# A macaron block on one core: the second batch's last shared-expert products, ahead of the expert tiles or inside them

## The chip, the cores and the metric

The kernel runs on one NeuronCore of a Trainium2 chip. The metric is the device time of one execution in microseconds; a kernel's time is the median of several executions. A core has TensorE (PE, matrix products), VectorE (DVE), ScalarE (ACT), GpSimd (POOL) and SyncE (SP), each with its own instruction queue; DMA engines move data between HBM and the on-chip memory. TensorE writes its results to PSUM, which has eight banks here.

## The reference

Input x has 4 batches of 512 rows with 256 columns, float32. Three half-steps follow one another, each on a layernorm without weights:

```
x = x + 0.5 * ffn(layernorm(x))
x = x + attention(layernorm(x))
x = x + 0.5 * ffn(layernorm(x))

ffn(x):   scores = sigmoid(x @ gate_w); the 2 best of 16 experts (by scores + bias), weights normed to sum 1
          shared = (silu(x @ shared_gate_w) * (x @ shared_up_w)) @ shared_down_w
          routed = sum over the two experts of weight * ((silu(g) * u) @ down[e]),  g, u = halves of x @ gate_up[e]
          return shared + routed
attention(x): 3 heads of 256; the softmax runs over the query axis; the heads' mean goes through fc_w, fc_b
```

There is one shared expert, which every row passes, and 16 routed experts with an inner width of 128. "Second shared expert" in the change's name is the shared expert on the second batch, x1.

## The kernel before

Rows are sorted by expert through memory. For each batch of 512 rows the kernel computes the layernorm, its transpose and the router's scores; finds for each row its two experts and its place among that expert's rows; and scatters the normed rows into a buffer `xn_d` in HBM, in which each expert has a region of its own (`router`, lines 359 to 445, GpSimd's indirect DMAs at line 438). Behind the last row of each region some blank rows are written (`blanks`, line 470). Then the routed experts run in tiles of 128 rows, all of one expert each: 40 tiles always, more only if the routing needs them.

`experts` (lines 621 to 699) is that loop, software-pipelined by hand. Step i does, in program order: load the rows of tile i (`load`, SyncE, line 569), transpose them on TensorE (`turn`, PSUM tile `pxt`, copied to `xt` by ScalarE); the gate and up products of tile i-1 (`up`, PSUM `peg`, with `sig` on ScalarE and two products on VectorE that give `eh`); the transpose of `eh` for tile i-2 (`flip`, PSUM `pht`, copied to `hT` by VectorE); the down product of tile i-3 (`down`, PSUM `pey`, scaled by ScalarE into `ey` and scattered to `y_d` in HBM by GpSimd, line 671). At given steps a function is called at the end of the step: the dictionary `at`. With the constants here, `DONE[0]` is 25, `late` is 37, and `NA[0]` is 40 tiles.

The first 9 tiles (`NF`) need only rows of the first three batches, so their table (`early`) is found before the last batch has been scattered. The table of the others is `table` (lines 547 to 559, on VectorE), and their loads wait for the blank rows.

The shared expert is three functions. `shared_up` (line 581): the two products of a batch, 128 x 512 each, in PSUM tiles `pg` and `pu` of tag "mm". `shared_gate` (line 594): two VectorE products, giving `h`. `shared_down` (line 600): four products of `h` with `shared_down_w` in two PSUM tiles `po` of tag "dn" (line 605; TensorE takes each float32 product in two passes, so the trace has 8 rows for it), and for each `po` one VectorE instruction that adds half of it to x (line 609). In the first half-step this is done for batches 0 and 1 ahead of the tiles, for batches 2 and 3 after them.

PSUM is shared out by tag: three banks for "mm" (`pg`, `pu`, `peg`, `pey`, the attention's products), three for "dn" (`pxt`, `pht`, `po`, the transposes of the layernorm), one each for the router's two. A tile gives its bank back when its last reader is done.

What sets the order. The framework's scheduler orders each engine's queue when the program is built: of the instructions that are ready it takes the first in program order. The kernel steers it in three ways. `in_turn` (line 224) ties groups of instructions on one engine, such as TensorE's groups ahead of the tiles, into a fixed sequence; "D0_1" is the name of the four products of `shared_down(1)`. `after` ties one instruction behind another of its engine; the argument `behind` of `shared_down` puts the VectorE sums of line 609 behind a given instruction. `tc.issue_after` does so for all that a block issues on that engine.

Before the change the order on VectorE at the end of the stage ahead is: `early`, `shared_gate(1)`, the two sums of batch 0, the two sums of batch 1, `table`. On TensorE it is: the groups C0_0 to C0_3 (counts), G2, Ug0_1 and Uu0_1 (`shared_up(1)`), D0_1, then the tiles.

Of the kernel before, what the change touches and what calls it, by code (L numbers as in the profile page):

```python
# [21 lines left out]
def tile_macaron_block(  # L22
# [51 lines left out]
    NA = [NK * NT + NE // 2, NK * NT + NE // 2 + 2]  # L74
# [141 lines left out]
    behind = const.tile([P, NB], F32, tag="behind", name="behind")  # L216
# [79 lines left out]
    class Ffn:  # L296
# [433 lines left out]
        def add(self, b, js=slice(0, NJ), behind=None):  # L730
            for yg in self.got[b]:
                ins = nc.vector.tensor_tensor(xs[b][:, js], xs[b][:, js], yg[:, js], ALU.add)  # L732
                if behind is not None:
                    after(ins, behind)


    ffn = Ffn(0)
# [68 lines left out]
        ffn.early()  # L806
    with tc.issue_after(ffn.last.ins):
        ffn.shared_gate(1)
    ffn.shared_down(0, behind=ffn.last)
    done = ffn.shared_down(1, behind=ffn.last)  # L810
    with tc.issue_after(done.ins):
        ffn.table()

    in_turn(
        "Z0", "Tln0_0", "Z1", "S0_0", "Tln0_1", "Z2", "K0_0", "Z3", "L0_0", "S0_1", "A0", "Ug0_0", "Uu0_0",
        "K0_1", "Tln0_2", "A1", "L0_1", "S0_2", "A2", "Tln0_3", "S0_3", "F", "K0_2", "L0_2", "G0",
        "D0_0", "G1", "K0_3", "L0_3", "C0_0", "C0_1", "C0_2", "C0_3", "G2", "Ug0_1", "Uu0_1", "D0_1",
    )

    in_turn(  # L820
# [8 lines left out]
    def add(f, b, j):  # L829
        return lambda: f.add(b, slice(j, j + 1), f.flips[-1])  # L830


    late = DONE[0] + 12
    ffn.experts(0, NA[0], {late - 10: ffn.ask, late: lambda: ffn.fetch_y(0)} | {
        late + 1 + j: add(ffn, 0, j) for j in range(NJ)
    })

# [201 lines left out]
    behind = ffn2.last  # L1039
# [39 lines left out]
```

## Time and profile before

| | |
|---|---|
| time, median of 4 runs | 509.76 us (507.44 to 510.96) |
| the profiled execution's own time | 512.11 us |
| its span, first to last instruction | 510.3 us |
| mean granted TensorE clock | 0.972 |
| stage ahead of the tiles | to about 57 us |
| first half-step's tiles | about 57 to 128 us |
| attention, three batches' routers in it | to about 400 us |
| second half-step's tiles | about 400 to 490 us |

In the profile's views, L605 is line 605 of the kernel; `po<-sd,h` names the tiles that an instruction writes and reads, without their numbers; x8 is the count of a merged row. The bracket behind a row is the idle time of that engine before it and what ended it. PE are TensorE's products, SPq the DMA queue that SyncE feeds, PEclk or the clock column the share of full clock that TensorE was granted. Ends of products are modelled: a product's row lasts longer than its share of a dense sequence, so the price of one in a sequence is taken from start to start.

### The profile page before, as it was taken

The page shows a single profiled execution, that of the slowest core. Times are in us where ns is not written, and L with a number is a line of the kernel's source. Part 1 is how long each engine was busy: PE and PEld are TensorE (multiplying, and loading weights), DVE is VectorE, ACT ScalarE, POOL GpSimd, SP SyncE. Part 2 cuts the span into 40 slices and gives each one's busy share as a digit, 9 for nine tenths or more (in the row PEclk, how much of TensorE's full clock was granted, in tenths as well). Part 3 has the DMA queues.
Part 4 walks back from the last instruction along what each step waited for, and adds up shares of the span by engine and source line. Part 5 has one row for each costly group of instructions (what it writes and reads, how often), then busy time and mean ns, then how long its engine had stood idle before and what let it go on. Part 6 is the DMA issues. An engine that isn't in the chain of part 4 may idle for free. (4 is left out here: it accounts for less than half of the span.)

```text
span 510.3 us, 7948 instructions
## 1 busy us (share of the span) xinstructions
PE 481.2 (94%) x2262; PEld 373.7 (73%) x2262; DVE 294.9 (58%) x981; ACT 224.5 (44%) x514; POOL 235.2 (46%) x281
## 2 busy tenths in 40 slices
PE   7988789999998999999999999999999889999985
PEld 3676478887566788678885778867888567888843
DVE  5856835556886922467406893325935475455565
ACT  3563256665436730456204664044640323666630
POOL 2377765665684140530256502644006067555543
PEclk9887999999999999999999999999999979999989
DMA  7996676566300000000022000200002327656756
GB/s 254 350 376 210 190 270 184 166 193 222 115 0 1 1 0 1 0 1 1 2 84 82 1 1 0 74 11 1 1 2 83 94 84 242 193 161 214 238 188 207
DMA packets 34734, 57.39 MB, mean 112 GB/s; under 512 B 4928, under 2 KB 25408, under 8 KB 34688
## 3 DMA queue, kind: packets, MB, share of 16 engines
q1 hardware_dynamic: 25424, 32.99, 21.3%
q0 software_dynamic: 8160, 23.44, 12.6%
q10 hardware_dynamic: 1104, 0.42, 0.3%
q8 instruction: 20, 0.33, 0.3%
q14 instruction: 26, 0.21, 0.2%
HBM read 30.78 MB, written 26.05 MB: 111 GB/s over the span
## 5 line engine op out<-in xcount | busy, mean ns | idle before, releaser
L671 POOL DMA_INDIRECT y_d<-ey,to x82 | 79.6, 970 | 53.6 <-ACT xt L632 43.3
L438 POOL DMA_INDIRECT xn_d<-xn_ln,pos x64 | 62.2, 972 | 86.6 <-DVE fa L489 23.0
L644 PE MATMUL peg<-gu,xt 128*128 x328 | 86.8, 389 | 3.0 <-DVE g L597 1.6
L970 PE MATMUL pa<-v,ex 128*128 128x256 f32 x384 | 86.2, 382 | 0.0
L970 PEld LDWEIGHTS pa<-v,ex 128*128 128x128 f32 x384 | 71.6, 190 | 9.2
L644 PEld LDWEIGHTS peg<-gu,xt 128*128 128x128 f32 x328 | 57.2, 194 | 10.3 <-issue 3.5
L661 DVE COPY hT<-pht 128x128 f32<-128x128 f32 x82 | 23.8, 290 | 55.2 <-PE pht L659 55.1
L666 PE MATMUL pey<-dn,hT 128*128 x164 | 49.3, 383 | 1.4 <-DVE hT L661 1.4
L670 ACT ACTIVATE ey<-pey,xg 128x256 f32<-128x256 f32 x82 | 38.9, 474 | 23.3 <-PE pey L666 21.8
L929 PE MATMUL pv<-G,xnT_lna 128*128 128x256 f32 x192 | 43.5, 382 | 2.7 <-ACT v L938 2.1
L868 PE MATMUL py<-xnT_lna,A 128*128 128x512 f32 x96 | 42.7, 593 | 1.0 <-DVEq L710 1.0
L929 PEld LDWEIGHTS pv<-G,xnT_lna 128*128 128x128 f32 x192 | 36.0, 190 | 9.6 <-ACT v L938 3.3
L905 ACT ACTIVATE ex<-ex,nmax 128x512 f32<-128x512 f32 x48 | 34.2, 714 | 18.5 <-DVE nmax L903 18.4
L650 ACT ACTIVATE sig<-peg 128x128 f32<-128x128 f32 x82 | 22.8, 278 | 41.4 <-PE peg L644 39.4
L975 DVE TENSOR_TENSOR x<-x,pa 128x256 f32<-128x256 f32 x16 | 6.7, 420 | 50.1 <-PE pa L970 45.3
L632 ACT COPY xt<-pxt 128x256 f32<-128x256 f32 x82 | 29.9, 366 | 12.0 <-PE pxt L628 8.8
L872 ACT COPY y<-py 128x512 f32<-128x512 f32 x24 | 13.8, 581 | 46.1 <-PE py L868 46.0
L628 PE MATMUL pxt<-ident,xg 128*128 128x128 f32 x164 | 31.8, 275 | 2.3 <-DVE xnT_ln L292 0.8
L868 PEld LDWEIGHTS py<-xnT_lna,A 128*128 128x128 f32 x96 | 18.2, 190 | 20.6 <-issue 19.8
L881 POOL TENSOR_TENSOR right<-y 128x256 f32<-128x256 f32 x12 | 10.0, 833 | 50.0 <-ACT y L872 50.0
L250 ACT ACTIVATE std_ln<-mv_ln,eps 128x4 f32<-128x4 f32 x8 | 2.4, 297 | 65.3 <-DVE mv_ln L248 65.2
L628 PEld LDWEIGHTS pxt<-ident,xg 128*128 128x128 f32 x164 | 22.5, 141 | 11.7 <-ACT xt L632 1.3
(201 smaller groups left out, 891.1 us busy)
## 6 DMA issues: line engine op xcount, KB each, us to landing
xg<-xn_d SPq DMA_DIRECT2D x82, 129.0 KB, 2.3
gu<-ffn_experts_gate_up_dram SPq DMA_DIRECT2D x4, 1024.0 KB, 14.2
yg<-y_d SPq DMA_DIRECT2D x8, 512.0 KB, 3.8
y<-y_d SPq DMA_DIRECT2D x6, 512.0 KB, 5.2
dn<-_L_ffn_experts_down_dram SPq DMA_DIRECT2D x2, 1024.0 KB, 15.2
x<-in_L_attn_x_dram SPq DMA_DIRECT2D x3, 512.0 KB, 7.8
out_dram<-x SPq DMA_DIRECT2D x3, 512.0 KB
y_d<-ey,to POOLq DMA_INDIRECT x82, 2.8
```

What stands on the lines that cost most here:

```text
L438: ins = nc.gpsimd.indirect_dma_start(out=self.xn_v[k * NT + b * NJ + j], out_offset=bass.IndirectOffsetOnAxis(ap=pos[:, k, j : j + 1], axi ...
L628: ins = nc.tensor.transpose(pt[:, c, :], xg[:, c * P : (c + 1) * P], ident)
L632: nc.scalar.copy(xt, pt)
L644: nc.tensor.matmul(pg, xt[:, c, :], gu[:, bass.ds(e, 1), c, :], start=(c == 0), stop=(c == NC - 1),)
L661: self.flips.append(nc.vector.tensor_copy(hT, pt))
L666: self.downed = nc.tensor.matmul(py, hT, dn[:, bass.ds(e, 1), :], start=True, stop=True)
L670: nc.scalar.mul(y, py, xg[:, H + 1 : W])
L671: ins = nc.gpsimd.indirect_dma_start(out=self.y_v[i], out_offset=bass.IndirectOffsetOnAxis(ap=tos[i], axis=0), in_=y, in_offset=None,)
L868: nc.tensor.matmul(py, A[h][:, c, fc * P : (fc + 1) * P], xnT[:, c, :], start=(c == 0), stop=(c == NC - 1),)
L905: nc.scalar.activation(ex[:, m, :], ex[:, m, :], AF.Exp, bias=nmax[:, m : m + 1], accum_out=z[:, m : m + 1],)
L929: nc.tensor.matmul(pv, xnT[:, c, m * P : (m + 1) * P], G[h][:, c, :], start=(c == 0), stop=(c == NC - 1),)
L970: nc.tensor.matmul(pa, es[h][:, m, j * P : (j + 1) * P], vs[h][:, m, :], start=(h == 0 and m == 0), stop=(h == NH - 1 and m == NJ - 1),)
```

## The change

The four products and the two VectorE sums of `shared_down(1)` are no longer issued ahead of the tiles. They are issued at the end of the tiles' step 34 (`late - 3`), the sums behind the copy `hT` that was issued last (`f.flips[-1]`, that of tile 32). The table now follows the sums of batch 0, and "D0_1" is no longer a member of the fixed TensorE sequence.

```diff
     with tc.issue_after(ffn.last.ins):
         ffn.shared_gate(1)
-    ffn.shared_down(0, behind=ffn.last)
-    done = ffn.shared_down(1, behind=ffn.last)
+    done = ffn.shared_down(0, behind=ffn.last)
     with tc.issue_after(done.ins):
         ffn.table()
...
-        "D0_0", "G1", "K0_3", "L0_3", "C0_0", "C0_1", "C0_2", "C0_3", "G2", "Ug0_1", "Uu0_1", "D0_1",
+        "D0_0", "G1", "K0_3", "L0_3", "C0_0", "C0_1", "C0_2", "C0_3", "G2", "Ug0_1", "Uu0_1",
     )
...
+    def down(f):
+        return lambda: f.shared_down(1, behind=f.flips[-1])
+
 
     late = DONE[0] + 12
-    ffn.experts(0, NA[0], {late - 10: ffn.ask, late: lambda: ffn.fetch_y(0)} | {
+    ffn.experts(0, NA[0], {late - 3: down(ffn), late - 10: ffn.ask, late: lambda: ffn.fetch_y(0)} | {
         late + 1 + j: add(ffn, 0, j) for j in range(NJ)
     })
```

No DMA, no buffer and no tile size changes; the sums are the same.

## The prediction

> **What bounds the kernel now.** I read the page first: the busy times and the row of slices.
>
> ```profile
> span 510.3 us, 7948 instructions
> PE 481.2 (94%) x2262; PEld 373.7 (73%) x2262; DVE 294.9 (58%) x981; ACT 224.5 (44%) x514; POOL 235.2 (46%) x281
> PEclk9887999999999999999999999999999979999989
> ```
>
> TensorE (PE) is busy 94% of the span, and its granted clock falls only in the stage ahead of the tiles and once near slice 32. An average says nothing of the two places that the change touches, so I read the timeline there. First the end of the stage ahead (start, duration, engine, line, tiles, count, and in brackets the idle time before and who ended it):
>
> ```profile
> 52.78 1.02 PE L587 MATMUL pu<-xnT_ln,su 128*128 128x512 f32 x2
> 54.46 5.32 SPq L569 DMA_DIRECT2D xg<-xn_d  x6
> 54.95 2.00 DVE L609 SCALAR_TENSOR_TENSOR x<-po,x 128x512 f32<-128x512 f32 x3
> 55.09 1.99 PE L605 MATMUL po<-sd,h 128*128 128x256 f32 x8 [1.28 <-DVE h L598]
> 57.12 0.69 DVE L609 SCALAR_TENSOR_TENSOR x<-po,x 128x512 f32<-128x512 f32 x1 [0.17 <-PE po L605]
> 57.15 0.41 PE L628 MATMUL pxt<-ident,xg 128*128 128x128 f32 x2
> 57.73 0.16 DVE L489 TENSOR_SCALAR na<-psr 128x16 f32<-128x16 f32 x1
> 57.90 0.41 PE L628 MATMUL pxt<-ident,xg 128*128 128x128 f32 x2 [0.34 <-DVE na L489]
> ```
>
> The row of 55.09 is the group that moves (D0_1). Of the four L609 instructions the last two are its own; the table (from L489 `na`) starts behind them. The first tile's rows were asked for at 54.46; the shortest landing of an `xg` in this stretch is 2.2 us, the median 2.6, so tile 0 could not begin before 56.66, and it began at 57.15. Then the two ends of the tile stage:
>
> ```profile
> SPq L569 <- DMA xn_d<-blank,end: 7.2, 1, 7.2
> 73.25 0.44 PE L628 MATMUL pxt<-ident,xg 128*128 128x128 f32 x2 [0.65 <-DMA xg<-xn_d]
> 76.00:100.00 24.00, 24.00 (x135) 20.23 (x134) 12.31 (x59) 14.84 (x45) 14.40 (x15) 1.00 0.59 173
> 114.47 0.38 PE L628 MATMUL pxt<-ident,xg 128*128 128x128 f32 x2
> 116.10 0.38 PE L628 MATMUL pxt<-ident,xg 128*128 128x128 f32 x2
> ```
>
> The first is from the waits of SyncE's queue: the load of tile 9, the first that needs the blank rows, waits 7.2 us for them, goes out at 71.01, and TensorE idles 0.65 us until 73.25. The blanks stand behind GpSimd's scatters, which follow one another every 1.27 us from 49.47 to 65.71 without waiting for DVE or TensorE. So tile 9 has an appointment that the change does not touch. From there TensorE is never idle (24.00 of 24.00 us, third row) and a step takes 116.10 - 114.47 = 1.63 us: **before tile 9 a saving is swallowed, behind it every TensorE microsecond counts**.
>
> **What leaves the stage ahead.** Eight TensorE rows (four float32 products, two passes each) and two L609. No DMA moves, and nothing of SyncE's or GpSimd's queue is passed. TensorE is free from 53.80, but tile 0 waits for its landing: a gain between 0 and 57.12 - 56.66 = 0.46 us; tile 1 began 0.34 us after TensorE could, about 2.4 us after its own load, so I take 0.2. The table starts two L609 earlier, 1.4 us, and so no longer stands in front of the second tile's `eh`: about 0.2 us. Both gains, 0.4, end in the appointment at 73.25: worth nothing by themselves.
>
> **What the stage ahead loses.** D0_1 was also the only dense TensorE work between 53.80 and 58.72, when the first tile's expert products start. Without it that stretch of 4.9 us holds two transposes of 0.41. Rows of this trace show what such a stretch does (windows: length, TensorE busy and count, granted clock, DMA share, GB/s; then the timeline):
>
> ```profile
> 36.00:38.00 2.00, 2.00 (x18) 1.00 1.06 374
> 38.00:40.00 2.00, 0.62 (x12) 0.52 1.10 389
> 40.00:42.00 2.00, 1.32 (x3) 0.50 1.06 362
> 56.00:58.00 2.00, 1.59 (x8) 1.00 0.79 222
> 40.68 3.78 PE L762 MATMUL pwG<-fcT,w 128*128 128x256 f32 x8 [2.06 <-ACT fcT L798]
> 46.30 1.89 PE L762 MATMUL pwG<-fcT,w 128*128 128x256 f32 x8
> ```
>
> After a few microseconds of small products and a 2.06 us pause the clock went to 0.50 and eight equal rows took 3.78 instead of 1.89 us. In windows of 0.4 us the half clock lasts 3.4 us once (31.2 to 34.6) and 6.8 us three times (10.7, 38.1, 410.1); the last began inside a pause of 1.55 us. So I expect the clock to fall around 56 to 59. Here a rule speaks against the change: the Trainium skill, "TensorE: Matmul & The Clock Gate", Part 1, says the clock halves after an idle window of about 3.4 us and recovers after a busy one, and its table of practice advises no idle gap above about 3 us. Taken literally it would leave 53.80 to 57.15 undecided at 3.35 us, so 0 or 1.7 us; the rows above are stricter, since pauses of 2.06 and 1.55 us among light work were enough.
>
> Price: 3.4 us at half clock, where TensorE has work throughout (58.7 to 62.0), cost 1.7 us of work; where it falls earlier, on time that TensorE waits away, 0.5 to 1. Against it stand the 0.4 gained and the 0.65 of waiting at tile 9: 1.7 - 1.05 = 0.65 at most for a single 3.4 us, nothing at least. For 6.8 us: 3.4 - 1.05 = 2.35. Ends 0 and 2.35; I take **0.45**, near the single window, as eight tiles of dense work follow.
>
> **What step 34 pays.** Eight rows at (1.89 - 0.38) / 7 = 0.216 us each are 1.73; the group's own row gives (1.99 - 0.38) / 7 = 0.23, 1.84. I take **1.75**, all on the path, at about 116.1, between step 34's `pey` and step 35's `pxt`. Nothing hides it: a step has no TensorE idle time. DVE takes two L609, 2 x 0.69 = 1.38; its own work in a step is 0.29 + 0.28 + 0.29 + 0.15 = 1.01 of 1.63, and a step of 3.4 us holds 2.4. Waits added: each L609 waits for its pair of products (the 0.17 above) behind the copy `hT` of tile 32; queued behind it on DVE are `sig`, `eh`, `to` and `hT` of the next tiles, for which TensorE would wait. The two `po` also hold two of three PSUM banks of tag "dn": the first is free 0.86 + 0.17 + 0.69 = 1.72 us after it starts, the second at about 1.73 + 0.17 + 0.69 = 2.6, while the flip of tile 33 and the transposes of tile 36 that take these banks come after 1.73 + 0.22 + 0.87 = 2.8 and 3.4. So nothing; at most 0.7, from the second half's shared expert inside tiles, where pxt at 425.32 to pxt at 436.06 is 10.74 us: three steps (4.88), its rows (3.43 + 1.71) and 0.7 of stall. x1 is next read at 135.10, so the later sum is late for nobody. All that follows (the adds behind flips 36 to 39, the layernorm, the attention) hangs on the tiles' end and shifts with it; the next batch's fetch at 119.45 waits for tile 30, ahead of step 34.
>
> **Sum.** -0.4 ahead, swallowed; +0.45 at tile 9 by the clock; +1.75 at step 34: **+2.2 us**. The profiled execution took 512.11 (510.3 span, 1.8 around it): 514.3. It lies 2.35 above the median of the runs, 509.76 (507.44 to 510.96), to which I carry the difference: **512.0**, 0.43% slower, within the 0.5% that a measurement can tell from no change.
>
> **The rivals.**
> - *The clock stays up* or its loss fits whole into the 0.65: +1.75, **511.5**. For: the landing may bring tile 0 early. Against: the light stretch is longer than those that cost the clock. 0.15.
> - *Slower*: the half clock lasts two windows, 6.8 us, as three of four times here; tile 9 is then over its appointment by 2.35, and with 1.75 that is +4.1, **513.9**; a bank stall of 0.7 would make 514.6. It decides from the point where tiles 0 to 8 lose more than 1.05 us. Against: dense tiles follow from 58.7. 0.18.
> - *The gain gets through*: the 0.46 + 0.2 + 0.65 reach the tile stage, if blanks land earlier because DVE and TensorE have less to do: 1.75 - 1.3 = +0.45, **510.2**. Against: GpSimd's even 1.27 us. 0.08.
> - *The products don't run at step 34*: only the DVE sums are tied to it, and the matmuls may be ordered into an earlier gap. Then they cost TensorE nothing, but hold two of three banks, and a step becomes 0.94 (`pxt` until its copy ends) + 0.60 (`pht`) + two handovers of 0.1, 1.74 instead of 1.63, for some 25 steps: 0 to +2.8, say **511.2**. Against: the third shared expert's L587 products, whose operands were copied by 35.9, passed no earlier tile and started at 128.54. 0.07.
>
> **How the numbers follow.** The forecast has 0.52, with +1.7 (511.5) to +2.9 (512.7). The range 509.6 to 514.3 takes in all rivals but the end of the slower one, and the scatter of the runs. Slower by over 0.5% (above 512.3): a third of the forecast, 0.17, and the slow rival, 0.18, with 0.02 of the last: 0.37. Faster by as much needs 507.2, which no case gives; 0.03 for what I don't see. The rest, 0.60, is within 0.5%.
>
> **What would show it.** After: L605 with eight rows near 116, pxt to pxt there 3.4 us; windows from 56 to 62 with a clock of 0.5; tile 9's pxt at 73.3 to 74, its idle time gone; `na` at about 56.3. I am wrong if the clock stays at 1.00, if tile 9 moves ahead of 73, or if the step with the products costs clearly more than 1.75.

## The result and the profile after

| | before | after |
|---|---|---|
| time, median | 510.06 us (507.14 to 513.58, 76 runs) | 512.09 us (510.52 to 515.95, 50 runs) |
| ratio | | 1.0037, 95% interval 1.0026 to 1.0048 |
| span of the profiled execution | 510.3 us | 509.3 us |
| mean granted TensorE clock of the runs | 0.979 (79 runs beside the experiments) | 0.973 |

By the ratio the change costs 1.9 us (1.3 to 2.4). The two profiled executions say the opposite, 510.3 and 509.3: one execution is not the kernel. The group `pg`, the first products of the second batch's shared expert, starts at 50.21 us in the one and at 47.45 in the other, before anything that the change touches. So all that follows is measured from this anchor inside the same execution, and only the medians of many runs are compared as totals. The anchor and the first expert products (`peg`) in TensorE's timeline of before:

```profile
50.21 1.88 PE L587 MATMUL pg<-xnT_ln,sg 128*128 128x512 f32 x4
...
58.72 1.10 PE L644 MATMUL peg<-gu,xt 128*128 x4 [0.41 <-ACT xt L632]
```

The page of the kernel after, in the rows that the prediction read:

```profile
span 509.3 us, 7948 instructions
...
PEclk9988899999999999999999999999999889999997
```

The instruction count is that of before, 7948; nothing was added or lost. The end of the stage ahead, from the timelines after the change:

```profile
47.45 1.88 PE L587 MATMUL pg<-xnT_ln,sg 128*128 128x512 f32 x4
...
51.62 7.49 SPq L569 DMA_DIRECT2D xg<-xn_d  x9
52.16 1.28 DVE L609 SCALAR_TENSOR_TENSOR x<-po,x 128x512 f32<-128x512 f32 x2
53.36 0.17 DVE L489 TENSOR_SCALAR na<-psr 128x16 f32<-128x16 f32 x1
53.75 0.44 PE L628 MATMUL pxt<-ident,xg 128*128 128x128 f32 x2 [2.70 <-DMA xg<-xn_d]
55.72 0.41 PE L628 MATMUL pxt<-ident,xg 128*128 128x128 f32 x2 [1.53 <-DVE tiles L559]
56.55 2.04 PE L644 MATMUL peg<-gu,xt 128*128 x4 [0.42 <-ACT xt L632]
```

Two L609 are left, the table's `na` follows them at once, and L605 is gone: TensorE waits 2.70 us for the first tile's rows and 1.53 for the second's. The second bracket names `tiles`, a result of the table, but in the kernel the transposes of the first nine tiles read nothing of the table. The second load went out at 52.49 and loads in this stretch landed after 2.1 to 4.3 us, which fits 55.72. Then the price: four `peg` rows take 2.04 us; before, four took 1.10. The windows of the same execution name the reason (length, TensorE busy and count, the other engines, granted clock, DMA share, GB/s), and the last row is the dense stretch behind tile 9:

```profile
56.00:58.00 2.00, 1.58 (x6) 1.21 (x5) 0.17 (x1) 0.37 (x1) 1.70 (x2) 0.51 0.97 239
58.00:60.00 2.00, 2.00 (x9) 1.63 (x8) 0.94 (x6) 0.65 (x2) 1.39 (x3) 0.64 0.95 268
...
76.00:100.00 24.00, 24.00 (x135) 20.29 (x134) 12.28 (x60) 15.08 (x45) 14.10 (x16) 1.00 0.59 174
```

The clock is at a half from 56 to 59.4 us, 3.4 us long; before it was 1.00 there. Tile 9, from SyncE's waits and TensorE's timeline:

```profile
SPq L569 <- DMA xn_d<-blank,end: 7.9, 1, 7.9
```

```profile
70.65 0.38 PE L628 MATMUL pxt<-ident,xg 128*128 128x128 f32 x2
...
113.37 1.89 PE L605 MATMUL po<-sd,h 128*128 128x256 f32 x8
115.10 0.38 PE L628 MATMUL pxt<-ident,xg 128*128 128x128 f32 x2
```

SyncE still waits for the blank rows, but TensorE no longer does: tile 9 at 70.65 has no bracket. From `pg` to tile 9 it took 23.20 us, before 23.04: the half clock ate what leaving out the products had given, and the 0.65 us that TensorE had waited at tile 9. At step 34 the eight rows of L605 stand where they were put; from their start to the next `pxt` is 115.10 - 113.37 = **1.73 us**. And VectorE in that step:

```profile
114.44 0.69 DVE L609 SCALAR_TENSOR_TENSOR x<-po,x 128x512 f32<-128x512 f32 x1 [0.42 <-PE po L605]
115.30 0.69 DVE L609 SCALAR_TENSOR_TENSOR x<-po,x 128x512 f32<-128x512 f32 x1 [0.17 <-PE po L605]
116.49 0.29 DVE L661 COPY hT<-pht 128x128 f32<-128x128 f32 x1 [0.50 <-PE pht L659]
```

VectorE is idle before the next copy: the sums hold nobody up. Tile 9 to tile 39 is 49.36 us before and 50.96 after; from tile 39 to the end of the span it is 387.69 in both. So from `pg` on this execution is 1.76 us longer: 0.16 ahead of tile 9, 1.60 between tiles 9 and 39, where step 34 is, and nothing behind.

### The profile page after: what moved, and what is told of

Same layout as the page of the kernel before. It is cut to its first block, busy times and chain, and to the rows that moved or that the text cites. A ratio compares the mean times of both kernels' runs of the same rounds, so it can differ in the third digit from the quotient of the medians.

```text
span 509.3 us, 7948 instructions
## 1 busy us (share of the span) xinstructions
PE 478.7 (94%) x2262; PEld 372.4 (73%) x2262; DVE 296.4 (58%) x981; ACT 224.4 (44%) x514; POOL 235.3 (46%) x281
## 3 DMA queue, kind: packets, MB, share of 16 engines
q1 hardware_dynamic: 25424, 32.99, 21.4%
## 5 line engine op out<-in xcount | busy, mean ns | idle before, releaser
L644 PE MATMUL peg<-gu,xt 128*128 x328 | 88.3, 394 | 2.3 <-DVE g L597 1.6
L874 ACT COPY y<-py 128x512 f32<-128x512 f32 x24 | 13.8, 581 | 46.1 <-PE py L870 46.0
## 6 DMA issues: line engine op xcount, KB each, us to landing
yg<-y_d SPq DMA_DIRECT2D x8, 512.0 KB, 4.1
y<-y_d SPq DMA_DIRECT2D x6, 512.0 KB, 4.7
x<-in_L_attn_x_dram SPq DMA_DIRECT2D x3, 512.0 KB, 7.1
out_dram<-x SPq DMA_DIRECT2D x3, 512.0 KB, 5.3
```

What stands on the lines that cost most here:

```text
L644: nc.tensor.matmul(pg, xt[:, c, :], gu[:, bass.ds(e, 1), c, :], start=(c == 0), stop=(c == NC - 1),)
```

## The experiments

The theory (T) in its final form at the start: ahead of the tiles the gain, tile 9's wait and the half clock about cancel; step 34 is paid in full. Rivals: the half clock is dear and step 34 cheap; or the half clock costs nothing; or the gain ahead could be had by moving the blank rows. This table holds all kernels that ran where the kernel before takes some 510 us: e10_base and e11_both_zero on one such chip, the other experiments on another, each experiment's ratio to the kernel before on the same chip. The segments come from the one profiled execution of each, the ratio and the mean clock from its timed runs (10 to 12 each, 50 of the kernel after).

| kernel | ratio to before, 95% | mean clock | half-clock windows of 3.4 us at tiles 0 to 4 | `pg` to tile 9 | idle at tile 9 | tile 9 to 39 |
|---|---|---|---|---|---|---|
| before | | 0.979 | 0 | 23.04 | 0.65 | 49.36 |
| after | 1.0037 (1.0026 to 1.0048) | 0.973 | 1 | 23.20 | 0 | 50.96 |
| e1_left_out | 1.0039 (1.0015 to 1.0063) | 0.974 | 2 | 24.67 | 0 | 48.94 |
| e2_extra | 1.0033 (1.0004 to 1.0062) | 0.979 | 0 | 22.98 | 0.55 | 50.96 |
| e11_both_zero | 1.0046 (1.0021 to 1.0071) | 0.978 | 0 | 22.09 | 0 | 50.95 |
| e3_warm | 1.0041 (1.0017 to 1.0066) | 0.978 | 0 | 23.65 | 1.04 | 51.07 |
| e10_base | 0.9994 (0.9968 to 1.0020) | 0.979 | 0 | 23.48 | 1.57 | 49.41 |
| e4_blanks_first | 1.0086 (1.0058 to 1.0114) | 0.975 | 1 | 26.33 | 0 | 48.82 |
| e12_step4 | 1.0028 (1.0001 to 1.0055) | 0.975 | 2 | 25.89 | 0 | 49.25 |
| e13_drain | 1.0061 (1.0035 to 1.0086) | 0.971 | 1 | 23.22 | 0.84 | 49.51 |

**Step 34 alone: e2_extra and e11_both_zero.** Both leave the products ahead of the tiles and issue them once more at step 34; in e2_extra both sums count, in e11_both_zero the sums ahead are multiplied by 0.0, so its values are those of the kernel after.

```diff
+    again = ffn.up[1]
     done = ffn.shared_down(1, behind=ffn.last)
+    ffn.up[1] = again
...
-    ffn.experts(0, NA[0], {late - 10: ffn.ask, late: lambda: ffn.fetch_y(0)} | {
+    ffn.experts(0, NA[0], {late - 3: down(ffn), late - 10: ffn.ask, late: lambda: ffn.fetch_y(0)} | {
```

> The kernel before, with the products and sums of shared_down(1) both ahead of the tiles and again at step 34, so that x1 gets the shared part twice: this times the step 34 part alone. My theory (eight rows at 0.216 us with nothing to hide them, no stall): +1.75 us against before, 1.70 to 1.85; clock 1.00 from 45 to 140 us, tile 9 still with its idle time. Rival, a PSUM bank or a VectorE wait in that step: +2.0 to +2.5 us. Rival, the step hides part of it: +0.5 to +1.3 us.

> The kernel after with the products of shared_down(1) also ahead of the tiles, where the kernel before has them, their sums there scaling by 0.0: the result is the kernel after's, and the difference from it is the stage ahead alone, with the same values. My theory (step 34 costs 1.73, the stage ahead about nothing): +1.5 to +2.0 us against before, mean clock as before (0.979), half clock absent from 56 to 62 us. Rival (the stage ahead costs 2 us, as e1_left_out had it): 0 to +0.5 us against before.

e2_extra took +1.7 us (0.2 to 3.2), e11_both_zero +2.3 (1.1 to 3.6), both at about the clock of before. TensorE's timeline of e11_both_zero:

```profile
113.94 1.89 PE L605 MATMUL po<-sd,h 128*128 128x256 f32 x8
115.67 0.38 PE L628 MATMUL pxt<-ident,xg 128*128 128x128 f32 x2
```

115.67 - 113.94 = 1.73 again. So step 34 costs 1.73 us with the stage ahead changed or not, and e11_both_zero, which has the step without the change ahead, is as slow as the kernel after: the stage ahead is worth 1.9 - 2.3 = -0.4 us, with an uncertainty of some 1.4 (both intervals together), which can't be told from nothing. The rival by which the stage ahead costs 2 us expected 0 to 0.5 here, and falls by this run; e1_left_out, below, fits it and stays unexplained.

**The clock alone: e3_warm.** Twelve products on constants behind the last `pu` keep TensorE busy where D0_1 had kept it busy.

```diff
+    warm = psum.tile([P, 512], F32, tag="rk", name="warm", bufs=1)
+    for _ in range(12):
+        mark("W", nc.tensor.matmul(warm, idle[:, 0:P], idle, start=True, stop=True))
...
-        "D0_0", "G1", "K0_3", "L0_3", "C0_0", "C0_1", "C0_2", "C0_3", "G2", "Ug0_1", "Uu0_1",
+        "D0_0", "G1", "K0_3", "L0_3", "C0_0", "C0_1", "C0_2", "C0_3", "G2", "Ug0_1", "Uu0_1", "W",
```

> The kernel after, with twelve products of 128x512 on constants (results unused) in the fixed sequence behind the second batch's up product, where the moved products stood: TensorE has dense work again from about 51 to 54 us. My theory: the clock stays at 1.00 around 56 to 59 us, and the loss ahead goes: +1.4 to +1.75 us against before, 0.1 to 0.65 us less than the kernel after. Rival, the half clock costs nothing because tile 9's wait swallows it: the same time as after, +1.9 us against before. Rival, the half clock of the kernel after is not due to the light stretch: the clock falls here too.

The clock came out as expected, the gain did not show. TensorE's timeline, then a window:

```profile
50.87 2.75 PE L811 MATMUL warm<-idle 128*128 128x512 bf16 x12
54.11 0.44 PE L628 MATMUL pxt<-ident,xg 128*128 128x128 f32 x2 [0.49 <-DMA xg<-xn_d]
55.99 0.41 PE L628 MATMUL pxt<-ident,xg 128*128 128x128 f32 x2 [1.45 <-DMA xg<-xn_d]
56.82 1.10 PE L644 MATMUL peg<-gu,xt 128*128 x4 [0.42 <-ACT xt L632]
```

```profile
56.00:58.00 2.00, 1.58 (x9) 1.23 (x10) 0.03 (x1) 0.41 (x2) 1.39 (x3) 1.00 0.87 274
```

The stretch is the same, the four `peg` rows are back at 1.10 us, the clock is at 1.00, and the twelve runs' mean clock is 0.978; so the light stretch without D0_1 is what had cost the clock. Yet the time is no better than that of the kernel after: +2.1 us (0.9 to 3.4), an interval that holds the +1.4 to +1.75 expected and the rival's +1.9 alike. In the profiled execution TensorE waits again at tile 9:

```profile
71.08 0.44 PE L628 MATMUL pxt<-ident,xg 128*128 128x128 f32 x2 [1.04 <-DMA xg<-xn_d]
```

So what the clock gave back is waited away. About half of that wait is chance: the load of tile 9 left 21.39 us after `pg` here, 20.86 in the kernel after.

**The part ahead alone: e1_left_out, e10_base.** e1_left_out lacks the second batch's shared part in x1; e10_base, which lacks it too, is the kernel before with the same values. First e1_left_out, from the kernel after, then e10_base, from the kernel before:

```diff
-    ffn.experts(0, NA[0], {late - 3: down(ffn), late - 10: ffn.ask, late: lambda: ffn.fetch_y(0)} | {
+    ffn.experts(0, NA[0], {late - 10: ffn.ask, late: lambda: ffn.fetch_y(0)} | {
```

```diff
-    done = ffn.shared_down(1, behind=ffn.last)
+    done = ffn.shared_down(1, behind=ffn.last, half=0.0)
```

> The kernel after, without the four products and the two sums of shared_down(1) at step 34: the second batch's shared expert is missing from x1, so this times the part of the change ahead of the tiles alone. My theory (the saving ahead is swallowed by tile 9's wait, and the light stretch costs a half clock of 3.4 us): +0.1 to +0.5 us against the kernel before, 1.73 us less than the kernel after; half clock near 56 to 59. Rival 1, the saving ahead gets through to the end: -0.5 to -1.3 us against before, and then step 34 cost more than its 1.75. Rival 2, two windows of half clock are usual: +1.5 to +2.4 us against before.

> e5_base_zero once more, since that ran on a chip on which the kernel before takes 538 us: the kernel before with the two sums of shared_down(1) scaling by 0.0, so that x1 lacks its shared part. Where the kernel before takes some 510 us: if the 2.0 us of e1_left_out come from other values of x1, this is +1 to +2 us against before. If they come from the stage ahead alone, it is 0 (-0.5 to +0.5).

e1_left_out took +2.0 us (0.8 to 3.2) against +0.1 to +0.5: a miss, and one that does not add up, since 2.0 ahead and 1.73 at step 34 would be 3.7, not 1.9. I supposed that the other values of x1 change the second half-step; e10_base (-0.3, -1.6 to +1.0), on the other chip, does not support that. The profile of e1_left_out is of the slowest of its twelve runs (515.48, median 512.21). There the first tile's rows came late (TensorE waited 3.81 us, 2.70 in the kernel after), two windows of half clock followed, from 59.2 to 66.0, and the tiles pay for both:

```profile
58.20 0.44 PE L628 MATMUL pxt<-ident,xg 128*128 128x128 f32 x2 [3.81 <-DMA xg<-xn_d]
...
62.54 3.61 PE L644 MATMUL peg<-gu,xt 128*128 x8
```

Eight `peg` rows took 3.61 us where 1.99 were usual; `pg` to tile 9 is 24.67, 1.5 us above the kernel after. Behind tile 39 this execution is another 1.6 us longer than the kernel after's: 0.4 in the attention, 0.9 in the second half-step's tiles, 0.3 behind them; no run shows why. The kernel after leaves +0.2 us (-0.4 to +0.7) for the stage ahead, e1_left_out's interval starts at 0.8. Why the median of twelve runs without the step is no lower than that of the kernel after is **left open**; no other run on a chip of 510 us repeats it.

**Moving the appointment: e4_blanks_first.** From before: GpSimd writes the blank rows ahead of the last batch's scatters.

```diff
     ffn.blanks()
+    for ins in ffn.scatters[B - 1]:
+        after(ins, ffn.blank[-1])
     ffn.loads()
```

> The kernel before, with the last batch's eight scatters tied behind the blanks on GpSimd; nothing else moves. My theory (tile 9 has an appointment with the blank rows, 0.65 us of TensorE idle): the load of tile 9 goes out several us earlier, the idle time at tile 9 is gone, -0.65 us against before, -0.3 to -0.8. Rival, the appointment is with something else (the last batch's scatters, which the load needs as well, now land later): 0 to +1 us, with the idle time still at tile 9 or at the next.

The idle time at tile 9 went, and the kernel lost 4.4 us (3.0 to 5.8), outside the theory's range and the rival's. TensorE's timeline:

```profile
56.57 0.41 PE L628 MATMUL pxt<-ident,xg 128*128 128x128 f32 x2 [1.84 <-DMA xg<-xn_d]
58.41 0.41 PE L628 MATMUL pxt<-ident,xg 128*128 128x128 f32 x2 [1.44 <-DMA xg<-xn_d]
```

The blanks now share the DMA engines with the loads of the first tiles: from issue to landing these took 3.9, 4.7, 5.6 us (least, median, most), in e2_extra 3.2, 3.5, 3.7, in nearly the same stretch. From 54 to 56 us the DMA engines moved 280 GB/s, in e2_extra 204. Tiles 0 and 1 wait 3.3 us in all, TensorE idles, and the clock halves here too, with D0_1 in its place. So the wait ahead of the dense work cost twice: itself, and the clock. And the load of tile 9 left only 1.7 us earlier after `pg` (19.15, before 20.80), since it also waits for the last batch's scatters, 1.8 us here. `pg` to tile 9 is 3.3 us longer than before; where the rest of the 4.4 goes this execution does not show, which is 2.6 us shorter than before's behind tile 9.

**Another place for the products: e12_step4, e13_drain.** At step 4, ahead of the appointment; or the two pairs at steps 40 and 41, where TensorE has gaps (`pair` is one `po` of `shared_down` with its sum, j the step less 38). Both from the kernel after:

```diff
-    ffn.experts(0, NA[0], {late - 3: down(ffn), late - 10: ffn.ask, late: lambda: ffn.fetch_y(0)} | {
+    ffn.experts(0, NA[0], {4: down(ffn), late - 10: ffn.ask, late: lambda: ffn.fetch_y(0)} | {
```

```diff
+    def also(j):
+        def both():
+            if j in (2, 3):
+                ffn.pair(1, 2 * (j - 2), ffn.flips[-1])
+            add(ffn, 0, j)()
+        return both
...
-        late + 1 + j: add(ffn, 0, j) for j in range(NJ)
+        late + 1 + j: also(j) for j in range(NJ)
```

> e7_step4 once more (products and sums at step 4 instead of 34), since e7_step4 ran on a chip on which the kernel before takes 538 us. Where the kernel before takes some 510 us: my theory (work ahead of tile 9 meets the appointment): 0 to +0.7 us against before. Rival, a product among the tiles is paid wherever it stands: +1.9 us. Where the stage ahead waits as on the chip of e7_step4, the products' going ahead of the tiles is worth 1 to 2 us, and the time is below before.

> The kernel after with the moved products split: the first pair at step 40 and the second at step 41, where no new tile comes in and TensorE stands idle for some 1.5 us in all, each with its sum behind the last hT. My theory (step 34 is paid because it is dense; the drain is not): 0 to +0.9 us against before, 1 to 1.7 us below the kernel after. Rival, the drain's idle time is already somebody's wait and the products push the shared expert of the third batch back by all of their 1.73 us: +1.9 us, as after. Rival, the sums hold the attention's layernorm up on VectorE by 1.4 us and that reaches TensorE: +2 to +3 us.

e12_step4 took +1.4 us (0.1 to 2.8), between the theory and its rival, and its interval holds values of both. Its profile has two windows of half clock, so TensorE was past the appointment (25.89 us after `pg`, no idle) when it came to tile 9, and in this execution the products were paid after all. The appointment swallows work only while TensorE is early.

e13_drain fell both ways. The drain did hide most: tile 39 to the third batch's `pg` is 6.47 us against 5.93, so 0.54 instead of 1.73. But it took +3.1 us (1.8 to 4.4). The attention shows where, in TensorE's timeline of e13_drain and a window:

```profile
161.15 2.04 PE L910 MATMUL psc<-right,xnT_lna 128*128 128x256 f32 x4 [2.56 <-ACT y L886]
```

```profile
162.00:164.00 2.00, 2.00 (x6) 1.55 (x6) 0.89 (x2) 1.56 (x2) 2.00 (x3) 0.50 0.00 0
```

The same wait for `y` is 1.79 us before; here it is 2.56, since VectorE's maximum in the softmax comes 0.8 us later against TensorE, and the clock halves behind it. What puts the maximum later is not shown. From tile 39 to the second half-step's first `pxt` it is 280.05 us, before 277.97. The last rival has this size, but it named the layernorm, which was in time against TensorE; in this execution a wait of the softmax 35 us later took the saving and more.

**On another chip.** Four kernels ran on a chip where the kernel before takes 538.17 us (534.92 to 544.18).

> The kernel before with every instruction in place, but the two sums of shared_down(1) scale their products by 0.0 instead of 0.5: x1 lacks its shared part, as in e1_left_out, and nothing else differs. It is the base for e1_left_out. My theory now (the missing rows of x1 change the second half-step's routing, and that made e1_left_out about 1 us longer behind the tiles): +0.5 to +1.5 us against before, and the tiles of the second half-step take some 60.8 us from tile 9 on instead of 59.6. Rival (values do not matter, and the stage ahead alone costs 2 us): 0 against before.

> e1_left_out once more, beside its base: the kernel after without the products and sums at step 34 (x1 lacks its shared part). My theory (ahead of the tiles the gain, the wait at tile 9 and the half clock about cancel): 0 to +0.7 us against e5_base_zero, with a mean clock some 0.005 lower. Rival, the half clock ahead costs what the whole change costs: +1.5 to +2.4 us against e5_base_zero.

> The kernel after with the products and sums issued at step 4 instead of step 34, all else equal. My theory (work ahead of tile 9 meets tile 9's appointment, work behind it is paid in full): +0 to +0.7 us against before, 1.2 to 1.8 us less than the kernel after. Rival, a product among the tiles is paid wherever it stands: +1.9 us, as after. Rival, a second window of half clock falls because the tiles start from a light stretch: +1.5 to +2.5 us.

> The kernel before with the table ahead of the two sums of shared_down(1) on VectorE; the products stay ahead of the tiles on TensorE. My theory (the table's earlier start ends in tile 9's appointment): -0.2 to +0.2 us against before, no clock lost around 56 to 59 us. Rival, the earlier table is a gain that gets through: -0.5 to -1.2 us. Rival, the sums now stand between the first tiles' VectorE work: +0.3 to +1 us.

e8_table_first issues `table` ahead of the two sums of the second batch, from before:

```diff
-    ffn.shared_down(0, behind=ffn.last)
-    done = ffn.shared_down(1, behind=ffn.last)
+    done = ffn.shared_down(0, behind=ffn.last)
     with tc.issue_after(done.ins):
         ffn.table()
+    ffn.shared_down(1, behind=ffn.last)
```

The ratios: e5_base_zero 1.0016 (0.9989 to 1.0042), e6_left_again 0.9974 (0.9952 to 0.9997), e7_step4 0.9986 (0.9957 to 1.0016), e8_table_first 0.9997 (0.9977 to 1.0017). e6_left_again, against its own base e5_base_zero, is 2.0 us faster (536.11 against 538.07) where 0 to +0.7 was expected, and e7_step4 lies 0.8 us below before (-2.3 to +0.9) where the theory had 0 to +0.7. These runs can't judge the theory, for the stage ahead is another there. TensorE in e5_base_zero:

```profile
74.86 3.46 PE L605 MATMUL po<-sd,h 128*128 128x256 f32 x8 [18.23 <-DVE h L598]
```

ScalarE, from which `h` hangs, stood 13.31 us ahead of 64.95 for nothing that the profile shows and 7.14 us more ahead of `g`, and D0_1 began behind 18.23 us of idle TensorE (1.28 where before takes 510 us). Tile 9 has no appointment left to keep there: the blanks were last issued at 68.68, tile 0 begins at 78.15, and no load waits for them. So work taken out ahead can get through, as e6_left_again's -1.4 us (-2.6 to -0.2) has it. What held ScalarE is open. That e8_table_first is unchanged fits the theory, but proves little on that chip.

## Why the prediction was right

Forecast +2.2 us to 512.0; measured +1.9 (1.3 to 2.4), 512.09. That the totals meet to 0.1 us is luck: the median before moved from 509.76 to 510.06 with more runs.

- **TensorE sets the end behind tile 9; right.** Tile 9 to 39 grows by about the products' price in every kernel that has it there (50.95 to 51.07 against 48.82 to 49.51).
- **Step 34, 1.75; right.** 1.73 in the kernel after and in e11_both_zero. The 0.7 of bank stall, kept as an end, did not come, and VectorE had room. The products ran at step 34, so the rival of an earlier gap was out.
- **The gain ahead, 0.4, swallowed; right in kind.** `na` came 5.91 us after `pg` instead of 7.52, 1.6 earlier for the 1.4 forecast; tile 0 came 6.30 after `pg` instead of 6.94, but 6.56, 6.62 and 7.41 in e12_step4, e13_drain and e1_left_out, so this part of the gain is not steady. Arriving early ends in a wait: 0.84 in e13_drain, 1.04 in e3_warm. The appointment itself moves too: with the blanks in their place the load of tile 9 left 19.9 to 21.4 us after `pg`, and e10_base, which moves nothing, waits 1.57, e11_both_zero not at all. The sign "tile 9 at 73.3 to 74" was wrong as an absolute time (70.65), for the whole stage moves by 3 us from one execution to the next; it should have been a distance from `pg`.
- **The clock; right in mechanism, mis-sized in its parts.** It fell where it was said, and the filled stretch held it (e3_warm). But I took one window as the usual case, 0.45 net, and gave two a chance of 0.18. Of the four profiles with the light stretch two show one window, two show two, and the runs' mean clock fits that, though it does not say where the clock was lost: (1 - 0.973) x 510 = 13.8 us of full clock missing after, 10.7 before, so 3.1 more, or 1.8 windows of 1.7. That is the slow rival's condition, without its price: 1.9 - 1.73 = +0.2 us (-0.4 to +0.7) is left for the whole stage ahead. Each came cheaper than written: one window cost +0.16 from `pg` to tile 9 (23.20 against 23.04) instead of 0.45, two +1.6 in e1_left_out instead of 2.35. That the sum came out is luck in this term: the second window is more frequent and the swallow larger than I had them, and the two errors offset each other; how they do so on average, e1_left_out leaves open.
- **The rule cited.** The Trainium skill, "TensorE: Matmul & The Clock Gate", Part 1, describes the window that decides as free-running and 3413 ns long. The runs agree: half clock, where the program's end does not cut it off, lasts 3.4 us, twice that, or in e1_left_out once four times that (11.4 to 25.2), at another place in each execution. The practice in the page's table "Why this matters for your kernels", no idle gap above some 3 us, is not enough: the clock halved here behind pauses of 2.70 and 1.53 us with two transposes, 0.44 us, between them, and in e13_drain behind one of 2.56.
- **The rivals.** The gain does not get through (ratio above 1); the clock does not stay up; the slow rival's 513.9 did not come in the median.

Two readings behind the clock's term were wrong. The prediction's count of half clocks before left out one, from 492.0 to 495.4, so two of five lasted 3.4 us, not one of four (a sixth is cut off by the end). And the clock fell at 38.05, ahead of the pause of 2.06 us (38.62 to 40.68) that the prediction names as a part of the cause. In the 3.4 us up to 38.05 TensorE has one pause in before's timeline, of 0.57 us; the rest are transposes and these short products of 16 columns each:

```profile
35.50 2.22 PE L335 MATMUL psr<-wr,xnT_ln 128*128 128x16 f32 x16 [0.57 <-ACT xnT_ln L288]
```

Nine of the ten profiles in the table have such a fall between 34 and 39 us with no pause above 0.57 us in the 3.4 us before it. So a light stretch did cost the clock, as the prediction says, but pauses alone do not tell which stretch is light.

## What to carry to other kernels

Find the next point at which the bounding engine waits for something that the change does not touch: as long as that wait is there, work taken out ahead of it gains little, while work put in behind it, where that engine has no gaps, is paid in full, 1.73 us for eight rows of 0.216. Before thinning a stretch ahead of dense work, count the pauses and the short products that it would leave: filling that stretch held the clock, and every kernel in the table that thinned it or made it wait lost clock. Compare two profiles by distances from an anchor within each, never by their spans.

## What the runs showed of the hardware

- Executions of the kernel before differ by 6.2 us (507.74 to 513.96 in 78 of the 79 runs beside the experiments; one took 515.87), with the mean clock between 0.970 and 0.988; the windows of half clock fall at other places in each profile. In the kernel before's execution their edges (10.75, 17.57, 31.2, 34.6, 38.05, 44.88, 410.1, 492.0) lie at multiples of 3.41 us from one another.
- A window of half clock need not cost time. From the first to the last `pxt` of the second half-step it took 84.1 us in e10_base with no window there, 83.1 in e3_warm with one, and 84.3 before with two. Over these 78 runs, though, the time is 0.26 us shorter for each 0.001 of mean clock (a straight line, correlation -0.78); 0.001 of 510 us is 0.51 us of full clock, so by this estimate about half of what the clock loses turns up as time.
- Chips differ by more than these kernels do: 510 and 538 us for the same program.
